# Two attention blocks: a stream's first two products interleaved, norm steps of the first attention issued later, factor operations of the projection spread over three products

## The chip, the core and the metric

The program runs on one core of a Trainium2 chip. The engines are named as the profile names them: PE (TensorE's matmuls) and PEld (its weight loads), DVE (VectorE), ACT (ScalarE), POOL (GpSimd) and SP (SyncE, which issues most of the transfers). The metric is the device time of one execution in microseconds, lower is better; a kernel's time is the median of its runs.

## The reference

The input x holds 8 images of 512 channels by 1024 positions (32 by 32), all in float32. Two layers follow each other, and each does the same five things for every image:

```
xn  = group_norm(x) * scale + bias            # 8 groups in layer 0, 32 groups in layer 1
q, k, v = qkv_w @ xn + qkv_b                  # three products of 512x512 with 512x1024
attn = softmax(q^T k / sqrt(64)) per head     # 8 heads of 64 channels
out  = attn applied to v                      # back to 512 x 1024
x    = proj_w @ out + proj_b + x              # the projection and the residual
```

## The kernel before, in words

**Units.** One layer of one image is a unit; there are 16, numbered u = 0 to 15, first the 8 images of layer 0, then those of layer 1. A unit makes v, q and k and runs its attention. The projection of a unit is done in the next unit, after that one's k; only the last is done by itself (`project_last`). Within unit u the order on PE is therefore: v, q, k of unit u, the projection o of unit u-1, the attention of unit u.

**Products in seven.** The products v, q, k and o are computed with seven block products in place of eight (2 by 2 blocks, a Strassen-like scheme), and each of these seven is again done as seven parts. `ORDER = (1, 6, 2, 7, 5, 4, 3)` is the order on both levels. The factors are sums and differences of blocks. For the weights they are stored in memory and loaded again; for the data side they are made in place by `Right.mix` (whole blocks, on DVE) and by `Right.quarter` and `Right.single` (four subtractions each, all recorded at L409: t1, t2, t4 and the in-place seventh, on POOL or DVE).

**The stream.** `Stream.product` (from L422) issues one block product. It uses two pairs of PSUM banks: a main pair (`apair[i]`, in the profile `a`), in which the four quarters q11, q12, q21 and q22 grow, and an auxiliary pair (`sbank[1-i]`, in the profile `s`), in whose bank 0 the running sum `one` grows, and in whose bank 1 lies the seventh part. i alternates from product to product. A quarter begins as a copy of `one` that ACT makes (`seed`, L444): q11 after part 1, q21 after part 6, q12 after part 5, q22 after part 4. The parts 2, 4 and 3 then add to q11, q21 and q12 (L436). ACT also copies the seventh part out of PSUM (`late`, L460); POOL adds it to results at the end (`add_late`, L480 and L489). The last two parts, 4 and 3, and the result's operations (`finish`) form a tail that is held back and issued by `close` inside the next product, after its part 1:

```
part(1, one, s, 0, True); seed(q11, 0)        # of this product
self.close()                                  # parts 4 and 3, seed q22 and finish, of the one before
part(6, ...); seed(q21, 1); part(2, ...); part(7, ...); copy late; part(5, ...); seed(q12, 0)
```

A part that adds to `one` must wait until ACT has read `one`; the parts of one product are so interleaved with the tail of the product before that another part stands between. The first product of a stream has no tail before it. There the kernel before issues the part 1 of the second product (`ahead`, only in `stream_values`) in that place, and the second product (`self.begun`) leaves its part 1 out.

**Hooks.** What DVE, POOL and SP do beside PE is placed by hand: `at(sel, k, ...)` hangs operations on the end of the result of product k of v, q, k or o. Each engine runs its instructions in the order in which they were issued. The factors of the projection are made during k: `o_part(5, ...)` are four DVE operations for the products 5 and 6 of the projection, of which `before` hangs two on k's product 7 and two on k's product 4; `o_part(4, ...)` are four POOL operations.

**Attention.** It has 64 steps (8 chunks of 8). In step s PE makes the scores (L807), ACT their exponentials (L815) into one of five tiles `p`, DVE sums those up (L852), and PE multiplies them with v (L835) one step later. Between chunks, DVE and ACT take the result out of the PSUM pair (L859, L861, L862), and DVE transposes and reduces the sums (L867, L875). `at_step` adds the group norm of the next unit: `aggregate`, `means` and `variances` (tiny matmuls, L283, into the pair that the next chunk will use, and DVE reads of them: L290 to L296, L301), the power on POOL (L303), `scales` (L308 to L318) and eight `apply` operations on ACT (L322). The steps are those of `USUAL` for u > 0 and of `LATE` for u = 0, where the input of unit 1 comes later and its statistics are taken in the attention too. `mixing` makes two of the next unit's factors on DVE (L219), `shadows` others on POOL, each tied to a summing operation of DVE. `rest_of_high` follows the attention and makes the rest of one pair's factors on POOL.

Of the kernel before, what the change touches and what calls it, by code (L numbers as in the profile page):

```python
# [11 lines left out]
F32 = mybir.dt.float32  # L12
# [6 lines left out]
P = 128  # L19
# [13 lines left out]
def fast_path(ctx, tc, x, qkv_wT, proj_wT, vecs, groups, out, flag):  # L33
# [217 lines left out]
    def halves(t):  # L251
        return [t[:, :, i : i + FD2] for i in range(0, t.shape[2], FD2)]
# [154 lines left out]
    def run(steps):  # L407
        for step in steps:
            step()  # L409

    class Stream:
# [10 lines left out]
        def product(self, a, b, keep, finish, tokens=False, ahead=None):  # L422
            i = self.n % 2
            self.n += 1
            main, aux, m, s = apair[i], sbank[1 - i], f"a{i}", f"s{1 - i}"
            one, seventh = aux[:, 0, :FD2], aux[:, 1, :FD2]
            q11, q12, q21, q22 = (main[:, r, ts(h, FD2)] for r in range(2) for h in range(2))

            def part(j, dst, tile_name, bank, start=False, a=a, b=b):
                for to, at, moving in (  # L430
                    [(dst[:, ts(i, P)], b[j][:, ts(i, P)], a[j]) for i in range(2)]
                    if tokens else [(dst, a[j], b[j])]
                ):
                    on(
                        "PE",
                        nc.tensor.matmul(  # L436
                            to, at, moving, start=start, stop=j != 1, skip_group_check=True
                        ),
                        tile_name, bank,
                    )  # L440
                    start = False

            def seed(dst, bank):
                n = nc.scalar.copy(dst, one)  # L444
                on("ACT", n, m, bank)
                on("ACT", n, s, 0)

            late = latepool.tile([P, FD2], F32, tag="late", name=f"late_{self.n}")
            if not self.begun:
                part(1, one, s, 0, True)  # L450
            self.begun = ahead is not None
            seed(q11, 0)
            if ahead is not None:
                part(1, sbank[i][:, 0, :FD2], f"s{i}", 0, True, *ahead)
            self.close()
            part(6, one, s, 0)
            seed(q21, 1)
            part(2, q11, m, 0)
            part(7, seventh, s, 1, not keep)
            on("ACT", nc.scalar.copy(late, seventh), s, 1)  # L460
            part(5, one, s, 0)
            seed(q12, 0)

            def tail():
                part(4, q21, m, 1)
                seed(q22, 1)
                part(3, q12, m, 0)
                finish(main, m, late)

            self.tail = tail  # L470
# [500 lines left out]
    def first_weights(after):  # L971
# [14 lines left out]
        "stats": (), "norm": (9, 11, 13, 16), "apply": (19, 20, 22, 23, 27, 28, 30, 31),  # L986
    }
    LATE = {
        "stats": (4, 5, 6, 7, 10, 11, 12, 13), "norm": (15, 19, 23, 26),
        "apply": (27, 28, 30, 31, 33, 35, 36, 38),  # L990
    }
    MAKING = (1, 2, 3, 4, 6)
    MAKE = {1: (1, "v"), 2: (1, "q"), 3: (1, "k"), 4: (1, "o")}
# [2 lines left out]
    for u in range(2 * B):  # L996
# [7 lines left out]
        def at(sel, k, *parts):  # L1004
            hooks.setdefault((sel, k), []).extend(parts)
# [50 lines left out]
        if u == 0:  # L1056
            def behind():
                for sel, bias, bank in (("q", QB, apair[0]), ("k", KB, sbank[1])):
                    run(block_steps(bank, lefts[sel].outer(1), right.outer[1], False, True, True))
                    t = early[sel] = ppool.tile([P, 2, FD], F32, tag="p", name=f"p1_{sel}_{u}")  # L1060

                    def copies(t=t, bank=bank, bias=bias):
                        for i in range(2):
                            nc.scalar.activation(
                                t[:, i, :], bank[:, i, :], AF.Identity, bias=vec[:, 0, bias, i : i + 1]
                            )

                    hooks[("v", 1)].insert(0, copies)

            (outer_q, inner_q), (outer_k, inner_k) = first["q"], first["k"]  # L1070
            hooks[("v", 1)].insert(1, partial(run, mixing_v[2:]))
            at("v", 6, partial(run, outer_q[:2]))
            at("v", 2, partial(run, outer_q[2:]))
            at("v", 7, partial(run, inner_q[:2]))
            at("v", 5, partial(run, inner_q[2:3]))
            at("v", 4, partial(run, inner_q[3:]), partial(store_image, 0, "q", slot_q))
            at("v", 3, partial(run, outer_k[:2]))
            at("q", 6, partial(run, outer_k[2:]))
            at("q", 2, partial(run, inner_k[:1]))
            at("q", 7, partial(run, inner_k[1:2]))  # L1080
            at("q", 4, partial(run, inner_k[2:3]))
            at("q", 3, partial(run, inner_k[3:]), partial(store_image, 0, "k", left_first_k))
            at("q", 3, partial(load_raw, 0, "o", slot_q))
            outer_o, inner_o = mix_left(slot_q)
            at("k", 7, partial(run, outer_o[:2]))
            at("k", 4, partial(run, outer_o[2:]))
            at("k", 3, partial(run, inner_o[:2]))
        else:

            (reciprocals, divide, *bias), (divide_2, *bias_2) = old.finish, old.before  # L1090
            ro = old.right_o
            o_parts = {}

            def o_rooms(ro=ro, parts=o_parts):
                tr = trpool.tile([P, 2, FD], F32, tag="tr", name=f"o_tr_{u}")
                oa, ob, oc = (ppool.tile([P, 2, FD], F32, tag="p", name=f"o{i}_{u}") for i in "abc")
                v, g = nc.vector, nc.gpsimd
                parts[1] = ro.quarter((1, 7), (*halves(tr), halves(oa)[0]), v)
                parts[5] = ro.quarter((5, 6), (halves(oa)[1], *halves(ob)), v)
                parts[2] = ro.quarter((2, 3), (*halves(oc), halves(xt[:, 1])[0]), g)  # L1100
                rooms = alone(xt[:, 1], 0, 1), alone(xt[:, 1], 1, 1), alone(xt[:, 0], 0, 0)
                parts[4] = ro.single(4, rooms, g)

            def o_part(k, lo=0, hi=4):
                return lambda: run(o_parts[k][lo:hi])

            transposed, reduced = old.sums
            at("v", 1, transposed)
            at("v", 2, reduced, divide_2)
            at("v", 4, reciprocals, bias_2[0])  # L1110
            at("v", 3, bias_2[1], o_rooms, partial(ro.mix, 0))
            at("q", 6, divide)
            at("q", 2, bias[0])
            at("q", 7, bias[1])
            at("q", 5, o_part(2, 0, 1))
            at("q", 4, partial(ro.mix, 3), o_part(2, 1, 2))
            at("q", 3, partial(ro.mix, 1))
            at("k", 1, partial(ro.mix, 2))
            at("k", 6, o_part(1, 0, 2), o_part(2, 2, 3))
            at("k", 2, o_part(1, 2), o_part(2, 3))  # L1120
            at("k", 7, o_part(5, 0, 2), o_part(4, 0, 2))
            at("k", 4, o_part(5, 2), o_part(4, 2))

        stream = Stream((u + 1) % 2)
        if u == 0:
# [48 lines left out]
        if not last:  # L1174
# [3 lines left out]
            )  # L1178
            shadows = {}
            if u == 0:  # L1180
                mixing[35], mixing[43] = partial(right.mix, 0), partial(right.mix, 1)
                parts = zip((40, 40, 42, 48, 48, 50, 56, 56), first_1 + first_6)
                parts = [*parts, *zip((58,), right.quarter((2, 3), (*halves(spare), halves(spare)[0]), nc.gpsimd))]
                for step, part in parts:
                    shadows.setdefault(step, []).append(part)
                shadows.update((at, [part]) for at, part in zip((8, 16, 24, 32), mix_left(slot_v, nc.gpsimd)[1]))
            else:
                mixing[27], mixing[35] = partial(right.mix, 0), partial(right.mix, 1)
                parts = zip((32, 32, 34, 40, 40, 42, 48, 48), first_1 + first_6)
                parts = [*parts, *zip((50, 56), right.quarter((2, 3), (*halves(spare), halves(spare)[0]), nc.gpsimd))]  # L1190
                for step, part in parts:
                    shadows.setdefault(step, []).append(part)
                if make is not None:
                    shadows.update((at, [part]) for at, part in zip((8, 16, 24), mix_left(left_slots[0], nc.gpsimd)[1][1:]))

            def rest_of_high(right=right):
                xb = ppool.tile([P, 2, FD], F32, tag="p", name=f"xb_{u + 1}")
                room, kept = halves(xb)
                run(right.quarter((2, 3), (*halves(spare), room), nc.gpsimd, kept)[1 if u == 0 else 2 :])

        making = [] if last else [None] * 8
        if make is not None:
# [332 lines left out]
```

## Time and profile before

| what | value |
|---|---|
| median of 3 runs | 3197.32 us (3197.13 to 3197.61) |
| the profiled execution, its own time | 3197.46 us |
| span of the profiled execution, first to last instruction | 3195.5 us |
| PE busy | 3170.3 us (99% of the span) |
| DVE, ACT, POOL busy | 2707.5, 2041.8 and 1257.3 us |
| mean granted TensorE clock | 0.999 |

A line of the timeline gives the start in us from the beginning of the span, the time until the last of its instructions ended, the engine, the line of the kernel, the operation, what is written and read, the shape, the number of instructions, and in brackets the idle time of the engine before it with what ended that. Matmuls are pipelined and their ends are modelled, so that the distance between two starts tells more of PE than the end of the first. A view of stretches gives the busy time of each engine with the number of its instructions, then the granted clock, the share of the DMA engines and GB/s.

### The profile page before, as it was taken

Reading aid. Unit: us, or ns where it says so; the run is one execution under the profiler, and the core shown is the slowest. Engines: PE = TensorE matmul, PEld = TensorE weight load, DVE = VectorE, ACT = ScalarE, POOL = GpSimd, SP = SyncE. Lnnn points to the kernel's source line nnn. Section 1 sums busy time; section 2 is a strip of 40 time slices with the busy share of each in tenths; the row PEclk is TensorE's granted clock in tenths of the full one; section 3 lists DMA queues with packets and bytes.
Section 4 is the critical chain, followed back from the end, with each engine's and each line's share of the span. In section 5 each row is a group of like instructions: output and inputs, shape, how many; then the busy total and the mean of one; then the engine's idle time right before and its main releaser. Section 6 shows DMA issues by size and latency. Waiting matters only on the chain.

```text
span 3195.5 us, 63766 instructions
## 1 busy us (share of the span) xinstructions
PE 3170.3 (99%) x24272; PEld 2016.2 (63%) x24272; DVE 2707.5 (85%) x3152; ACT 2041.8 (64%) x3572; POOL 1257.3 (39%) x965
## 2 busy tenths in 40 slices
PE   9999999999999999999999999999999999999999
PEld 7466484765847658476584755748567485674843
DVE  7988989889798897888979888798897988879877
ACT  3665767666676666766667666676666766667664
POOL 5145162452714427054361533615336162351620
PEclk9999999999999999999999999999999999999999
DMA  4334343443434324233142331423314233243311
GB/s 175 103 117 147 115 149 94 162 129 115 161 105 147 120 63 162 79 119 127 56 167 79 121 119 56 167 79 132 108 56 168 89 127 101 67 167 91 131 59 49
DMA packets 155270, 365.81 MB, mean 114 GB/s; under 512 B 30160, under 2 KB 45776, under 8 KB 154960
## 3 DMA queue, kind: packets, MB, share of 16 engines
q1 hardware_dynamic: 154672, 361.53, 33.9%
q8 instruction: 197, 3.23, 0.4%
q14 instruction: 113, 0.93, 0.1%
q10 hardware_dynamic: 288, 0.13, 0.0%
HBM read 299.72 MB, written 59.77 MB: 112 GB/s over the span
## 4 chain that ended last, share of the span: by engine, by line
PE 93%; DVE 4%; ACT 1%; issue 1%; DMA 0%; POOL 0%; SPq 0%; ACTq 0%; DVEq 0%; POOLq 0%
PE a L835 27%; PE s L807 25%; PE s L436 22%; PE a L436 16%; PE a L807 1%; DVE acc L852 1%; DVE ob L409 1%; ACT a L444 1%; DVE u_k L523 1%; PE s L753 0%; PE a L753 0%; PE a L409 0%; DVE oa L409 0%; DVE k L562 0%; DVE u_k L533 0%
## 5 line engine op out<-in xcount | busy, mean ns | idle before, releaser
L815 ACT ACTIVATE p<-s 128x1024 f32<-128x1024 f32 x976 | 997.0, 1023 | 524.4 <-PE s L807 499.8
L835 PE MATMUL a<-p,v 64*64 64x512 f32 x8192 | 1098.2, 590 | 4.2 <-DVE var L301 2.1
L807 PE MATMUL s<-q,k 64*64 64x512 f32 x7808 | 1056.3, 591 | 0.0
L852 DVE TENSOR_TENSOR acc<-acc,p 128x1024 f32<-128x1024 f32 x768 | 953.6, 1242 | 76.4 <-ACT p L815 35.1
L444 ACT COPY a<-s 128x256 f32<-128x256 f32 x1728 | 614.3, 358 | 326.6 <-PE s L436 220.5
L835 PEld LDWEIGHTS a<-p,v 64*64 64x64 f32 x8192 | 379.9, 131 | 505.0 <-ACT p L815 353.4
L807 PEld LDWEIGHTS s<-q,k 64*64 64x64 f32 x7808 | 377.9, 133 | 438.0 <-issue 438.0
L460 ACT COPY late<-s 128x256 f32<-128x256 f32 x432 | 160.8, 372 | 227.5 <-PE s L436 219.0
L436 PE MATMUL s<-k,w 128*128 128x256 f32 x672 | 195.2, 379 | 0.5 <-ACT a L444 0.5
L852 DVE TENSOR_TENSOR acc<-p,p 128x1024 f32<-128x1024 f32 x128 | 156.0, 1219 | 9.4 <-ACT p L815 9.4
L1249 POOL TENSOR_TENSOR k<-xn 128x256 f32<-128x256 f32 x15 | 11.0, 731 | 375.5 <-PE s L807 246.8
L867 DVE STREAM_TRANSPOSE tr<-acc 128x1024 f32<-128x1024 f32 x128 | 157.9, 1234 | 0.0
L875 DVE TENSOR_REDUCE red<-tr 128x32 f32<-128x1024 f32 x128 | 154.0, 1203 | 0.0
L436 PE MATMUL a<-xn,w 128*128 128x256 f32 x492 | 146.3, 379 | 0.0
L436 PE MATMUL a<-xt,w 128*128 128x256 f32 x462 | 137.5, 379 | 0.0
L436 PEld LDWEIGHTS s<-k,w 128*128 128x128 f32 x672 | 125.0, 190 | 19.2 <-ACT a L444 1.3
L303 POOL TENSOR_TENSOR y<-var,half 128x4 f32<-128x4 f32 (+1 forms) x17 | 17.6, 1035 | 287.4 <-DVE var L301 287.4
L862 DVE TENSOR_TENSOR ao<-a,tmp 128x512 f32<-128x512 f32 x128 | 87.9, 687 | 48.7 <-ACT tmp L861 48.1
L480 POOL TENSOR_TENSOR q<-q,late 128x512 f32<-128x512 f32 x64 | 98.4, 1537 | 62.8 <-ACT a L444 45.4
L489 POOL TENSOR_TENSOR v<-v,late 128x512 f32<-128x512 f32 x60 | 89.7, 1495 | 59.9 <-DVE v L590 35.8
L436 PE MATMUL s<-xn,w 128*128 128x256 f32 x372 | 110.7, 379 | 0.0
L436 PE MATMUL s<-xt,w 128*128 128x256 f32 x372 | 110.6, 379 | 0.0
(259 smaller groups left out, 5140.7 us busy)
## 6 DMA issues: line engine op xcount, KB each, us to landing
w<-iq SPq DMA_DIRECT2D x105, 448.0 KB, 3.4
w<-ik SPq DMA_DIRECT2D x105, 448.0 KB, 7.1
w<-io SPq DMA_DIRECT2D x105, 448.0 KB, 6.8
w<-iv SPq DMA_DIRECT2D x98, 448.0 KB, 3.9
rb<-drec SPq DMA_DIRECT2D x128, 256.0 KB, 3.9
xn<-mid SPq DMA_DIRECT2D x36, 512.0 KB, 3.6
xn<-x_dram SPq DMA_DIRECT2D x32, 512.0 KB, 3.8
res<-x_dram SPq DMA_DIRECT2D x32, 512.0 KB, 6.1
```

What stands on the lines that cost most here:

```text
L436: nc.tensor.matmul(to, at, moving, start=start, stop=j != 1, skip_group_check=True),
L444: n = nc.scalar.copy(dst, one)
L460: on("ACT", nc.scalar.copy(late, seventh), s, 1)
L480: return nc.gpsimd.tensor_add(cols, cols, twice(late))
L489: return nc.gpsimd.tensor_add(cols, cols, parts)
L807: nc.tensor.matmul(bank[e * H : (e + 1) * H, j, :], w.k[pr][j * H : (j + 1) * H, t * P + e * H : t * P + (e + 1) * H], w.q[pr][j * H : (j ...
L815: exp = nc.scalar.activation(p, bank, AF.Exp, scale=SCALE)
L835: nc.tensor.matmul(banks[r][j * H : (j + 1) * H, :], w.v[rows, t, lo : lo + D], p[rows, j, :], start=(t == 0), stop=(t == NT - 1),)
L852: state["sums"].append(nc.vector.tensor_add(acc, state["first"] if t == 1 else acc, p))
L862: i1 = nc.vector.tensor_add(ao[:, pr, ts(qh, FD)], banks[1], tmp)
L867: nc.vector.transpose(tr, state["acc"].pop(c))
L875: nc.vector.tensor_reduce(red[:, :, qh, :], state["tr"].rearrange("p j (f i) -> p j f i", i=BL), AX.X, ALU.add)
```

## The change

Three things are changed, and no instruction of the program is added or removed by them.

First, `Stream.product` has three orders in place of one. In the first product of `stream_values` (it gets `ahead`) the order is: part 1, part 7, part 1 of the second product, seed q11, copy late, part 6, seed q21, part 2, part 7 of the second product, seed q11 of the second product, part 5, seed q12. In the second product (`begun`) it is: part 6, seed q21, then the tail of the first (`close`), part 2, copy late, part 5, seed q12. All other products keep their order.

Second, for u = 0 the norm steps `means`, `variances` and `scales` come at steps 20, 27 and 30 instead of 19, 23 and 26, and the eight `apply` at 32 to 44 instead of 27 to 38. The two `mixing` operations go from 35 and 43 to 43 and 51, the eight POOL operations that follow from them from 40 to 56 to 48 to 58, and a ninth POOL operation that was tied to step 58 goes into `rest_of_high`.

Third, of the four DVE operations `o_part(5, ...)` the first stays at k's product 7, the second goes to product 4 (which keeps the third), and the fourth goes to product 3.

```diff
+            late = latepool.tile([P, FD2], F32, tag="late", name=f"late_{self.n}")
...
-            def seed(dst, bank):
+            def seed(dst, bank, one=one, m=m, s=s):
                 n = nc.scalar.copy(dst, one)
                 on("ACT", n, m, bank)
                 on("ACT", n, s, 0)
 
-            late = latepool.tile([P, FD2], F32, tag="late", name=f"late_{self.n}")
-            if not self.begun:
+            def keep_late():
+                on("ACT", nc.scalar.copy(late, seventh), s, 1)
+
+            if ahead is not None:
+
+                other, its_one, its_seventh = f"s{i}", sbank[i][:, 0, :FD2], sbank[i][:, 1, :FD2]
                 part(1, one, s, 0, True)
-            self.begun = ahead is not None
-            seed(q11, 0)
-            if ahead is not None:
-                part(1, sbank[i][:, 0, :FD2], f"s{i}", 0, True, *ahead)
-            self.close()
-            part(6, one, s, 0)
-            seed(q21, 1)
-            part(2, q11, m, 0)
-            part(7, seventh, s, 1, not keep)
-            on("ACT", nc.scalar.copy(late, seventh), s, 1)
-            part(5, one, s, 0)
+                part(7, seventh, s, 1, not keep)
+                part(1, its_one, other, 0, True, *ahead)
+                seed(q11, 0)
+                keep_late()
+                part(6, one, s, 0)
+                seed(q21, 1)
+                part(2, q11, m, 0)
+                part(7, its_seventh, other, 1, True, *ahead)
+                seed(apair[1 - i][:, 0, :FD2], 0, its_one, f"a{1 - i}", other)
+                part(5, one, s, 0)
+                self.begun = True
+            elif self.begun:
+                self.begun = False
+                part(6, one, s, 0)
+                seed(q21, 1)
+                self.close()
+                part(2, q11, m, 0)
+                keep_late()
+                part(5, one, s, 0)
+            else:
...
             seed(q12, 0)
...
     LATE = {
-        "stats": (4, 5, 6, 7, 10, 11, 12, 13), "norm": (15, 19, 23, 26),
-        "apply": (27, 28, 30, 31, 33, 35, 36, 38),
+        "stats": (4, 5, 6, 7, 10, 11, 12, 13), "norm": (15, 20, 27, 30),
+        "apply": (32, 33, 36, 38, 39, 41, 43, 44),
     }
...
-            at("k", 7, o_part(5, 0, 2), o_part(4, 0, 2))
-            at("k", 4, o_part(5, 2), o_part(4, 2))
+            at("k", 7, o_part(5, 0, 1), o_part(4, 0, 2))
+            at("k", 4, o_part(5, 1, 3), o_part(4, 2))
+            at("k", 3, o_part(5, 3))
...
             if u == 0:
-                mixing[35], mixing[43] = partial(right.mix, 0), partial(right.mix, 1)
-                parts = zip((40, 40, 42, 48, 48, 50, 56, 56), first_1 + first_6)
-                parts = [*parts, *zip((58,), right.quarter((2, 3), (*halves(spare), halves(spare)[0]), nc.gpsimd))]
+                mixing[43], mixing[51] = partial(right.mix, 0), partial(right.mix, 1)
+                parts = zip((48, 48, 50, 56, 56, 56, 58, 58), first_1 + first_6)
...
-                run(right.quarter((2, 3), (*halves(spare), room), nc.gpsimd, kept)[1 if u == 0 else 2 :])
+                run(right.quarter((2, 3), (*halves(spare), room), nc.gpsimd, kept)[0 if u == 0 else 2 :])
```

The `else` branch holds the order of before, word for word but for `keep_late()`.

More of the change, by code (lines that the diff above doesn't have):

```diff
@@ L446, in seed @@
                 on("ACT", n, s, 0)
-            late = latepool.tile([P, FD2], F32, tag="late", name=f"late_{self.n}")
-            if not self.begun:
+            def keep_late():
+                on("ACT", nc.scalar.copy(late, seventh), s, 1)
+            if ahead is not None:
+                other, its_one, its_seventh = f"s{i}", sbank[i][:, 0, :FD2], sbank[i][:, 1, :FD2]
                 part(1, one, s, 0, True)
-            self.begun = ahead is not None
-            seed(q11, 0)
-            if ahead is not None:
-                part(1, sbank[i][:, 0, :FD2], f"s{i}", 0, True, *ahead)
-            self.close()
-            part(6, one, s, 0)
-            seed(q21, 1)
-            part(2, q11, m, 0)
-            part(7, seventh, s, 1, not keep)
-            on("ACT", nc.scalar.copy(late, seventh), s, 1)
-            part(5, one, s, 0)
+                part(7, seventh, s, 1, not keep)
[18 more added lines that the diff above has]
+            else:
+                part(1, one, s, 0, True)
+                seed(q11, 0)
+                self.close()
+                part(6, one, s, 0)
+                seed(q21, 1)
+                part(2, q11, m, 0)
+                part(7, seventh, s, 1, not keep)
+                keep_late()
+                part(5, one, s, 0)
             seed(q12, 0)
```

## The prediction

> **What bounds the kernel now.** I read the page's busy times first, then the list of waits for PE, then the timelines of three places that PE's starts point to.
>
> ```profile
> PE 3170.3 (99%) x24272; PEld 2016.2 (63%) x24272; DVE 2707.5 (85%) x3152; ACT 2041.8 (64%) x3572; POOL 1257.3 (39%) x965
> ```
>
> PE sets the time: whatever closes a hole between its matmuls is won whole, and nothing else is. The waits of PE say where holes are:
>
> ```profile
> PE s L436 <- ACT a L444: 4.2, 17, 0.5
> PE a L835 <- DVE var L301: 2.1, 1, 2.1
> PE a L835 <- ACT p L815: 2.0, 1, 2.0
> ```
>
> These are too small, as ends of matmuls are modelled; I go by starts. First place, the start of a stream (unit 3; PE, then the ACT copy that it waits for):
>
> ```profile
> 595.20 0.71 PE L436 MATMUL s<-w,xn 128*128 128x128 f32 x4
> 595.75 0.61 PE L436 MATMUL s<-w,xt 128*128 128x128 f32 x4
> 596.50 0.68 PE L436 MATMUL s<-w,k 128*128 128x128 f32 x4
> 597.02 0.61 PE L436 MATMUL a<-w,xn 128*128 128x128 f32 x4
> ...
> 598.36 0.61 PE L436 MATMUL a<-w,k 128*128 128x128 f32 x4
> 599.03 0.71 PE L436 MATMUL a<-w,xn 128*128 128x128 f32 x4
> ...
> 601.36 0.61 PE L436 MATMUL s<-w,xn 128*128 128x128 f32 x4
> ...
> 596.00 0.36 ACT L444 COPY a<-s 128x256 f32<-128x256 f32 x1 [2.10 <-PE s L436]
> ```
>
> A part (a line here) takes 0.447 us when nothing waits (597.02 to 598.36 are three of them). The twelve parts from 595.20 to 601.36 should take 5.36, plus 0.10 for the slow first one, and take 6.16: 0.70 is lost. Of it 0.38 lie at 596.50 (part 6 waits until ACT has read `one`, then restarts slowly) and 0.32 at 599.03 (part 3 waits for seed q12). All 15 streams of u > 0 show it: 0.70 in thirteen, 0.98 in units 11 and 12.
>
> Second place, the end of k (unit 3; DVE, ACT, PE):
>
> ```profile
> 653.91 0.67 DVE L409 TENSOR_TENSOR oa<-ot 128x512 f32<-128x512 f32 x1
> 654.62 1.64 DVE L409 TENSOR_TENSOR ob<-ot,oa 128x512 f32<-128x512 f32 x1
> 656.18 0.68 DVE L533 TENSOR_TENSOR u_k<-a,u_k 128x512 f32<-128x512 f32 x1
> 656.78 0.67 DVE L562 TENSOR_TENSOR k<-a,u_k 128x512 f32<-128x512 f32 x1
> ...
> 657.55 0.63 ACT L444 COPY a<-s 128x256 f32<-128x256 f32 x2 [0.68 <-DVE k L562]
> ...
> 657.17 0.59 PE L436 MATMUL a<-xt,w 128*128 128x256 f32 x2
> 657.96 0.70 PE L436 MATMUL s<-spare,w 128*128 128x256 f32 x2 [0.19 <-ACT a L444]
> ```
>
> PE needs 0.43 per part here; 657.17 to 657.96 is 0.79, and the next part starts 0.10 late: 0.46 lost. Backwards: seed q11 of product 3 waits for DVE to read product 5's bank 0 (L562), which queues behind the second factor operation, 1.64 us long. This too stands in each of the 15 units.
>
> Third place, the attention of u = 0 (PE, ACT, then a view of stretches):
>
> ```profile
> 125.84 1.13 PE L807 MATMUL s<-q,k 64*64 64x512 f32 x8
> 129.11 1.09 PE L835 MATMUL a<-p,v 64*64 64x512 f32 x8 [2.14 <-DVE var L301]
> ...
> 135.14 1.07 PE L807 MATMUL s<-q,k 64*64 64x512 f32 x8
> 138.24 1.47 PE L835 MATMUL a<-p,v 64*64 64x512 f32 x8 [2.03 <-ACT p L815]
> ...
> 136.37 0.81 ACT L322 ACTIVATE xn<-xn,shift,scale 128x512 f32<-128x512 f32 x1 [2.51 <-DVE shift L318]
> ...
> 138.00:143.00 5.00, 4.76 (x30) 1.93 (x34) 3.94 (x5) 3.19 (x5) 0.00 (x0) 0.66 0.01 3
> ```
>
> From its first scores to the next stream this attention takes 116.87 us, the others 110.26 to 110.35: 6.5 lost. 2.4 are the products of step 24, whose bank DVE has not yet read for the variances; 2.2 the exponential behind an `apply` that waits for `shift`; 1.7 a stretch of half clock right after (granted 0.66 over 138 to 143); 0.2 later.
>
> **The parts and their costs.**
>
> *Stream start.* No instruction is added. Copy to refill: part 1 starts at 595.20, ACT copies at 596.00 for 0.36, PE resumes at 596.50, so 1.30 after part 1's start (1.20 for later parts). Now two parts stand between (7 and the other 1): part 6's turn comes at 0.10 + 3 x 0.447 = 1.44. Part 5's copy feeds part 3 two parts later in the same way, margin 0.14. The new seed q11 of the second product stands in ACT's queue behind seed q21: part 6 starts at 1.44, seed q21 runs 2.14 to 2.50, the new one to 2.86, PE may go on at 3.00, its turn is at 3.23. That copy writes the pair that DVE empties last (L859, L862); they end 1.55 after the stream's start in every unit, 0.95 before it is due. Behind it in ACT's queue are q12, q21, q22 and the copy of v's first result; all keep at least 0.1. So 0.70 x 15 = 10.5 gained; the extra 0.28 of units 11 and 12 I leave as noise (11.1 with it). Unhidden at worst: one of the hops again, about 0.3 per start, 4.5.
>
> *Factor operations.* The 1.64 us operation moves from before product 5's result to after product 4's. L533 then starts when product 5's tail is done, near 654.8, not 656.18. L562 also needs POOL's add to u_k (done 655.71 by its row, 654.07 for 1.64), so bank 0 is read by 656.5, and the ACT copy is due at 656.9, after part 1 of product 3. The hole of 0.46 closes: 15 units sum to 7.0. What is later: L409 twice after product 4's result (ends 658.9), then product 3's result, then the fourth operation. They take 0.67 alone and up to 1.75 beside POOL (its adds are 1.27 each). Two such give 662.4 at worst, against 662.25, where product 3's result stands now, and the copy of the projection's product 6 that needs this result comes near 664.2. The fourth operation ends by 665.5 at worst; its reader, part 7 of that product 6, comes near 661.1 - 0.46 + 3.02 + 5 x 0.43 = 665.8. All is covered, by 0.3 at worst, 1.9 if no POOL operation is in the way. Cost 0, bounds -0.46 (the gain eaten) and 0 per unit.
> The Trainium skill, page "SBUF — State Buffer", section "Who interferes with whom", says a DVE instruction with two SBUF inputs and a GpSimd one that reads SBUF block each other for a whole instruction; 0.67 against 1.64 to 1.75 in this trace agrees. By that rule all three moved operations could draw the long time, the worst case just given.
>
> *First attention.* Matmul of the means one step later: DVE reads them before the products of step 25, since its pair is free until then. Variances at step 27, in chunk 3, use the pair of chunk 4, whose products start at step 33: the 2.4 goes. DVE, however, is behind by 3 us and stays the clock of `scales`. From its rows: sums 1.33 apart, 1.14 before another operation, reciprocals 1.56, transposition 1.16, reduction 1.13, divide 1.14, means 0.54. From step 20's sum (121.93): means at 123.07, step 24's evacuation at 128.9, sum of step 27 at 134.4, variances 135.5 (step 33's products come after 140: free), step 30's sum 139.2, `shift` done 141.35. Step 32's scores come at 124.08 + 8 x 1.718 = 137.82, its exponential ends at 140.0, the evacuation copy at 140.54, so `apply` waits 0.8 for `shift`, ends 142.2, the next exponential 143.1, and products that were due at 142.1 start at 143.3: 1.15 lost, with two more `apply` in a row 0.15. So 6.5 - 1.3 = 5.2 gained; bounds 6.5 (DVE catches up, ACT alone costs little) and 2.5 (DVE 1 us later and half clock again).
> The Trainium skill, page "TensorE: Matmul & The Clock Gate", section "What's actually happening", has the clock halved after an idle window of about 3.4 us; here two idles of about 2.2, neither of that length, came before the 0.66, so the trace is stricter. By the page one hole of 1.15 leaves the clock whole, as I took it.
> `mixing` and POOL's work come later in u = 0. The last eight small operations (0.74 each) end near step 60, before unit 1 reads them. The ninth starts without its tie: DVE sums beside POOL rows take 2.11 in place of 1.23 (192 to 199), one or two more of them use up DVE's idle 1.06 before L859 of unit 1. I take 0.3, bounds 0 and 1.0.
>
> *Sum.* Against the profiled execution's own 3197.46 (span 3195.5 and 1.96 around it, 0.14 above the median): -10.5 - 7.0 - 5.2 + 0.3 = -22.4, 3175.1. Against the median it is 3174.9; I say 3175.0.
>
> **Rivals.**
> 1. *The first attention still jams.* For: DVE's backlog, and step 32 puts evacuation copy and `apply` on ACT together. Against: the variance read is off the path. Gain 2.5 or less, worst none: 3177.7 to 3180.5.
> 2. *DVE and POOL block each other, and product 3's result or the fourth factor comes late:* the 0.46 moves into the projection. For: the 0.3 margin at worst. Against: POOL must draw first three times. 3182.
> 3. *The streams keep one hop,* as margins of 0.14 are thin. Against: the ordinary products run on the same margin without holes. 10.5 - 4.5 gained: 3179.5.
> 4. *Slower than before:* the new seed q11 is issued before q12 and the rest on ACT; if it waits for more of DVE than the emptying, all behind it waits. It decides when DVE's release comes later than 2.6 after the start (then part 6 of the second product is late), and turns the sum when it costs 22.4/15 = 1.5 per start, so at 4.1. If it waited for the first factor of the next mix (L219, ends 5.15), 2.5 x 15 = 38: 3213. Against: L862 ends at 1.55 fifteen times.
> 5. *Nothing changes,* as PE waits elsewhere for the same engines: 3197.
>
> **Chances.** Forecast 0.62 (3173 to 3177.5), rival 1 0.15, rival 2 0.09, rival 3 0.08, rival 4 0.04, rival 5 0.02. The low end takes all bounds: 11.1 + 7.1 + 6.5 = 24.7, 3172.5. The high end includes rivals 1 to 3: 3182.5. Within 0.2% (6.4 us, about what a measurement here can tell from no change) is rival 5 and the edge of 4: 0.03; slower 0.04; faster 0.93.
>
> **What would show it.** After: PE's streams start their second `s<-w,xn` after 5.46, with no idle before parts 6 and 3; at the end of k no ACT wait for L562, `ob` after L551; the first attention near 111.6 with one wait for ACT around step 33, none for var, and no stretch under full clock. Wrong if the streams still take 6.16, if a hole of 0.4 opens in the projection, or if unit 0 keeps more than 114.

## The result, and the profile after

The changed kernel takes 3176.12 us (median of 4 runs, 3175.14 to 3177.38) against 3197.23 (3196.84 to 3197.61) for the kernel before: a ratio of 0.9934, 95% interval 0.9917 to 0.9951. The forecast was 3175.0, with a range from 3172.5 to 3182.5. The profiled execution has a span of 3175.5 us, 20.0 less than that of before. A second series (e10_after below) gave 3174.88, ratio 0.9932 (0.9918 to 0.9946).

The page's first part, of the changed kernel:

```profile
PE 3159.3 (99%) x24272; PEld 2027.4 (64%) x24272; DVE 2686.2 (85%) x3152; ACT 2043.6 (64%) x3572; POOL 1261.4 (40%) x965
```

The same instructions on every engine, as the diff says. The waits of PE, those that answer to the three of before:

```profile
PE a L858 <- ACT p L838: 2.3, 1, 2.3
PE s L437 <- ACT a L445: 1.9, 3, 0.9
```

The wait for `var` is gone. Of 17 waits of `s` for ACT's copies three are left (L437 is the old L436, L445 the old L444, L858 the old L835, L838 the old L815, L830 the old L807, L875 the old L852, L882 and L885 the old L859 and L862, L574 and L585 the old L551 and L562).

The start of a stream, unit 3, PE in order of time (start, time until the last ended, what, how many):

```profile
591.61 1.16 PE L437 MATMUL s<-w,xn 128*128 128x128 f32 x8
592.61 0.61 PE L437 MATMUL s<-w,xt 128*128 128x128 f32 x4
593.05 0.61 PE L437 MATMUL s<-w,k 128*128 128x128 f32 x4
593.50 0.61 PE L437 MATMUL a<-w,xn 128*128 128x128 f32 x4
593.95 1.50 PE L437 MATMUL s<-w,k 128*128 128x128 f32 x12
595.29 0.61 PE L437 MATMUL a<-w,k 128*128 128x128 f32 x4
595.73 0.61 PE L437 MATMUL a<-w,xn 128*128 128x128 f32 x4
...
597.07 0.61 PE L437 MATMUL s<-w,xn 128*128 128x128 f32 x4
```

The first line is parts 1 and 7 together, the fifth parts 7 (of the second product), 5 and 6 (of the second). From 591.61 to the third product's first part at 597.07 it takes 5.46 us, where it took 6.16: not one start is late. The end of k, unit 3, DVE and PE:

```profile
649.63 0.68 DVE L409 TENSOR_TENSOR oa<-ot 128x512 f32<-128x512 f32 x1
650.49 0.69 DVE L556 TENSOR_TENSOR u_k<-a,u_k 128x512 f32<-128x512 f32 x1 [0.19 <-PE a L437]
651.10 0.68 DVE L585 TENSOR_TENSOR k<-a,u_k 128x512 f32<-128x512 f32 x1
...
653.63 1.23 DVE L574 TENSOR_TENSOR k<-a,u_k 128x1024 f32<-128x1024 f32 x1 [0.65 <-PE a L437]
654.77 0.68 DVE L409 TENSOR_TENSOR ob<-ot,oa 128x512 f32<-128x512 f32 x1
655.49 1.64 DVE L409 TENSOR_TENSOR ob<-ot,ob 128x512 f32<-128x512 f32 x1
657.05 1.21 DVE L574 TENSOR_TENSOR k<-a,u_k 128x1024 f32<-128x1024 f32 x1
658.18 0.77 DVE L409 TENSOR_TENSOR ot<-ot 128x512 f32<-128x512 f32 x1
...
652.88 0.64 PE L437 MATMUL a<-xt,w 128*128 128x256 f32 x2
653.36 0.59 PE L437 MATMUL s<-spare,w 128*128 128x256 f32 x2
```

Product 5's result (L556, the old L533) now waits for PE and no longer behind the factor operation; L585 reads bank 0 by 651.78. On PE 652.88 to 653.36 is 0.48 where it was 0.79. Of the three operations that now stand at the products 4 and 3, all of which run beside rows of POOL, one took 1.64 (the others 0.68 and 0.77), here and in the 14 other units.

The first attention: PE, then ACT and one line of DVE, then three stretches (length, busy time and instructions of PE, PEld, DVE, ACT and POOL, granted clock, DMA share, GB/s):

```profile
142.13 1.13 PE L830 MATMUL s<-q,k 64*64 64x512 f32 x8
145.57 1.09 PE L858 MATMUL a<-p,v 64*64 64x512 f32 x8 [2.31 <-ACT p L838]
...
140.78 0.58 ACT L884 COPY tmp<-a 128x512 f32<-128x512 f32 x1
143.70 0.81 ACT L322 ACTIVATE xn<-xn,shift,scale 128x512 f32<-128x512 f32 x1 [2.34 <-DVE shift L318]
144.42 1.00 ACT L838 ACTIVATE p<-s 128x1024 f32<-128x1024 f32 x1
...
125.53 0.59 DVE L914 TENSOR_REDUCE tot<-lt 32x64 f32<-32x256 f32 x1 [0.98 <-DMA lt<-red]
```

```profile
138.00:143.00 5.00, 5.00 (x51) 2.36 (x42) 4.86 (x8) 2.52 (x3) 2.00 (x1) 1.00 0.02 3
143.00:148.00 5.00, 2.69 (x28) 1.12 (x28) 4.90 (x9) 4.30 (x6) 2.10 (x1) 1.00 0.00 0
148.00:153.00 5.00, 5.00 (x52) 2.10 (x48) 4.79 (x5) 4.22 (x6) 0.00 (x0) 1.00 0.06 12
```

One hole is left, at step 33 and for the reason given: `apply` on ACT waits for `shift`. The clock stays whole. This execution lost 2.5 us there; 1.0 of it is DVE's wait for a landing (`lt<-red`), which is absent in the other profiles of this order. From its scores to the next stream this attention took 112.84 us here and 111.78 in e10_after, against 116.87 before.

What the forecast had too small stands at the start of unit 1, DVE, POOL, ACT and PE:

```profile
191.50 8.25 DVE L875 TENSOR_TENSOR acc<-acc,p 128x1024 f32<-128x1024 f32 x4
199.67 0.68 DVE L882 COPY tmp<-a 128x512 f32<-128x512 f32 x1
200.38 0.69 DVE L885 TENSOR_TENSOR ao<-a,tmp 128x512 f32<-128x512 f32 x1
...
191.99 2.26 POOL L409 TENSOR_TENSOR spare<-xn 128x512 f32<-128x512 f32 x1
194.32 2.14 POOL L409 TENSOR_TENSOR spare<-xn,spare 128x512 f32<-128x512 f32 x1
196.54 2.13 POOL L409 TENSOR_TENSOR xb<-xn,spare 128x512 f32<-128x512 f32 x1
198.63 2.25 POOL L409 TENSOR_TENSOR xb<-xn 128x512 f32<-128x512 f32 x1
...
201.11 0.63 ACT L445 COPY a<-s 128x256 f32<-128x256 f32 x2 [1.38 <-DVE ao L885]
...
201.52 0.71 PE L437 MATMUL s<-w,k 128*128 128x128 f32 x4 [0.90 <-ACT a L445]
```

DVE's last four sums take 8.25 us beside four operations of POOL. So DVE empties the pair 3.85 us after the stream began (200.38 + 0.69 - 197.23), the copy q11 of the second product waits for that, and PE loses 1.16 there and 1.0 more in v. Unit 1 takes 198.30, the usual unit 196.08.

One hole stands in every unit of the kernel before and of the changed one alike. PE at the end of unit 3's projection:

```profile
675.81 0.59 PE L437 MATMUL s<-oc,w 128*128 128x256 f32 x2
676.24 0.59 PE L437 MATMUL a<-xt,w 128*128 128x256 f32 x2
676.85 0.70 PE L437 MATMUL a<-ao,w 128*128 128x256 f32 x2
```

From 676.24 to 676.85 it takes 0.61 in place of 0.43, and the last part restarts 0.10 late: 0.28 lost. The order is part 5, copy q12, part 4, part 3, with one part between the copy and the part that adds to it, as in the second hole of the old stream start. In the 15 units with a projection it adds up to 4.2 us, and no run here changes it.

### The profile page after: what moved, and what is told of

The parts are those of the page before. It is cut to its first block, busy times and chain, and to the rows that moved or that the text cites. A ratio compares the mean times of both kernels' runs of the same rounds, so it can differ in the third digit from the quotient of the medians.

```text
span 3175.5 us, 63781 instructions
## 1 busy us (share of the span) xinstructions
PE 3159.3 (99%) x24272; PEld 2027.4 (64%) x24272; DVE 2686.2 (85%) x3152; ACT 2043.6 (64%) x3572; POOL 1261.4 (40%) x965
## 4 chain that ended last, share of the span: by engine, by line
PE 97%; DVE 1%; DMA 0%; issue 0%; ACT 0%; SPq 0%; DVEq 0%; ACTq 0%
PE a L858 27%; PE s L830 26%; PE s L437 23%; PE a L437 18%; PE a L830 1%; DVE acc L875 1%; PE s L776 0%; PE a L776 0%; PE a L409 0%; PE s L345 0%; PE s L409 0%; DVE w L409 0%; DMA xn<-x_dram 0%; DMA rb<-drec 0%; DMA drec<-rec 0%
## 5 line engine op out<-in xcount | busy, mean ns | idle before, releaser
L838 ACT ACTIVATE p<-s 128x1024 f32<-128x1024 f32 x976 | 997.2, 1023 | 520.7 <-PE s L830 497.7
L858 PE MATMUL a<-p,v 64*64 64x512 f32 x8192 | 1100.4, 589 | 2.3 <-ACT p L838 2.3
L830 PE MATMUL s<-q,k 64*64 64x512 f32 x7808 | 1058.6, 590 | 0.0
L875 DVE TENSOR_TENSOR acc<-acc,p 128x1024 f32<-128x1024 f32 x768 | 955.7, 1244 | 75.8 <-ACT p L838 32.9
L445 ACT COPY a<-s 128x256 f32<-128x256 f32 x1728 | 616.1, 358 | 324.1 <-PE s L437 225.2
L858 PEld LDWEIGHTS a<-p,v 64*64 64x64 f32 x8192 | 382.6, 131 | 499.1 <-ACT p L838 353.4
L830 PEld LDWEIGHTS s<-q,k 64*64 64x64 f32 x7808 | 383.5, 133 | 431.5 <-issue 431.5
L437 PE MATMUL s<-k,w 128*128 128x256 f32 x672 | 195.3, 380 | 0.5 <-ACT a L445 0.5
L875 DVE TENSOR_TENSOR acc<-p,p 128x1024 f32<-128x1024 f32 x128 | 156.1, 1220 | 9.0 <-ACT p L838 9.0
L437 PE MATMUL a<-xn,w 128*128 128x256 f32 x492 | 146.5, 379 | 0.0
L437 PE MATMUL a<-xt,w 128*128 128x256 f32 x462 | 137.5, 379 | 0.0
L437 PEld LDWEIGHTS s<-k,w 128*128 128x128 f32 x672 | 125.1, 190 | 19.1 <-ACT a L445 1.3
L885 DVE TENSOR_TENSOR ao<-a,tmp 128x512 f32<-128x512 f32 x128 | 88.1, 688 | 48.7 <-ACT tmp L884 48.2
L437 PE MATMUL s<-xn,w 128*128 128x256 f32 x372 | 110.7, 379 | 0.0
L437 PE MATMUL s<-xt,w 128*128 128x256 f32 x372 | 110.7, 379 | 0.0
L322 ACT ACTIVATE xn<-xn,shift,scale 128x512 f32<-128x512 f32 x124 | 99.5, 804 | 14.2 <-DVE shift L318 14.2
```

The lines of the kernel that those rows point to most:

```text
L322: nc.scalar.activation(cols, cols, AF.Identity, bias=st["shift"][:, c - lo : c - lo + 1], scale=st["scale"][:, c - lo : c - lo + 1],)
L437: nc.tensor.matmul(to, at, moving, start=start, stop=j != 1, skip_group_check=True),
L830: nc.tensor.matmul(bank[e * H : (e + 1) * H, j, :], w.k[pr][j * H : (j + 1) * H, t * P + e * H : t * P + (e + 1) * H], w.q[pr][j * H : (j ...
L838: exp = nc.scalar.activation(p, bank, AF.Exp, scale=SCALE)
L858: nc.tensor.matmul(banks[r][j * H : (j + 1) * H, :], w.v[rows, t, lo : lo + D], p[rows, j, :], start=(t == 0), stop=(t == NT - 1),)
L875: state["sums"].append(nc.vector.tensor_add(acc, state["first"] if t == 1 else acc, p))
```

## The experiments

**The three parts by themselves.** Each is the kernel before with one part of the diff: the new `product` and no more, the three lines of `o_part(5, ...)` and no more, the `LATE`, `mixing`, `parts` and `rest_of_high` lines and no more.

> The kernel before with the new stream order alone. My theory: the two holes of each stream (0.38 and 0.32) close in all 15 units, unit 1 too, because without the later POOL work of unit 0 DVE empties the pair in time: 10.5 to 11.1 us less than before, 3186.2 to 3186.7 against a before of 3197.2. The rival (the copy q11 of the second product waits for DVE, which empties that pair last): a hole like the 1.06 us one of unit 1 would stand in more units, 3188 or more. Streams should take 5.46 us from the first part to the third product's first part.

> The kernel before with the projection's factor operations over three products alone. My theory: the hole of 0.46 at the end of k closes in all 15 units and nothing opens in the projection: 7.0 us less, 3190.2. The rival (DVE and POOL block each other, and the hole moves on): 3197 or up to 3194, with holes of some tenths in the projection.

> The kernel before with the later norm steps of the first attention alone (with their later mixing and POOL operations). From the changed kernel's trace: the attention of unit 0 loses 2.5 in place of 6.5, 4.0 won; unit 1 starts with DVE 2.3 us late, which in the old stream order costs nothing at the copy q11 of the second product (it is due later there) but about 0.9 in v: 3.1 less, 3194.1. If instead the 2.1 us that unit 1 lost belong to the norm steps whatever the stream order, 1.9 less, 3195.3. If half clock returns, 1.7 more.

| kernel | median (runs) | before, same chips | ratio (95%) | what its profile shows |
|---|---|---|---|---|
| e1_stream | 3186.10 (6) | 3197.5 (27) | 0.9965 (0.9952 to 0.9977) | a usual unit 196.55 (197.25 before); no hole at any of the 15 starts |
| e2_factors | 3189.41 (10) | 3197.5 (27) | 0.9976 (0.9966 to 0.9985) | a usual unit 196.78; no hole at the end of k, and in the projection only the 0.28 at its end that before has too |
| e3_norm | 3193.76 (10) | 3197.5 (27) | 0.9989 (0.9980 to 0.9999) | attention of unit 0 111.81, with one hole of 1.5; unit 1 198.35, 1.0 more than before |

The three gains are 11.4, 8.1 and 3.7 us by the medians, 23.2 together, where the whole change gave 21.1 and 22.7 in its two series. By the profiles the 15 starts take 11.3 less (93.2 to 81.9), the factor operations gain 7.1, the norm steps 4.1. For e1_stream that agrees with the theory, unit 1 included: without the later norm steps the pair is emptied in time there. For e3_norm, too, the first of the two accounts holds: the norm steps cost unit 1 1.0 us in the old order of the stream, and 1.4 to 2.2 together with the new one.

**Half of the interleave.** In the kernel before, only the first product's part 7 is moved:

```diff
             seed(q11, 0)
             if ahead is not None:
+                part(7, seventh, s, 1, not keep)
                 part(1, sbank[i][:, 0, :FD2], f"s{i}", 0, True, *ahead)
...
             part(2, q11, m, 0)
-            part(7, seventh, s, 1, not keep)
+            if ahead is None:
+                part(7, seventh, s, 1, not keep)
```

> The kernel before, but the first product of a stream issues its part 7 second; the second product keeps its old order. My theory of two separate holes: the one ahead of part 6 closes (0.38), the one ahead of part 3 stays (0.32): 15 x 0.38 = 5.7 less, 3191.5, and 5.78 from a stream's first part to the third product. The rival, that the first hole is only passed on to the second: same as before.

3195.38 us (10 runs), ratio 0.9993 (0.9983 to 1.0003): the expected 5.7 did not come. PE at the start of unit 5 of this kernel:

```profile
990.15 1.16 PE L436 MATMUL s<-w,xn 128*128 128x128 f32 x8
991.14 0.61 PE L436 MATMUL s<-w,xt 128*128 128x128 f32 x4
991.59 0.61 PE L436 MATMUL s<-w,k 128*128 128x128 f32 x4
992.04 0.61 PE L436 MATMUL a<-w,xn 128*128 128x128 f32 x4
992.70 0.71 PE L436 MATMUL s<-w,k 128*128 128x128 f32 x4
993.25 0.61 PE L436 MATMUL a<-w,k 128*128 128x128 f32 x4
993.92 0.71 PE L436 MATMUL a<-w,xn 128*128 128x128 f32 x4
...
996.25 0.50 PE L436 MATMUL s<-w,xn 128*128 128x128 f32 x3
```

The hole ahead of part 6 is closed (991.14 to 991.59), but a new one has opened ahead of part 5 (992.04 to 992.70, 0.32 with its slow restart), and the one ahead of part 3 stays (993.25 to 993.92). Part 7 had been the second of the two parts that cover the copy q21; taken away, it was missed there. The start takes 6.10 instead of 6.16. So the rival came close to the truth, by another way than it said: the copies q11, q21 and q12 each need two parts of 0.447 between. The change gives q21 its second only because the second product's part 7 takes the place that the first one's left, and q12 its second by the second product's part 6.

**Is the third product needed?** The changed kernel with the fourth factor operation on product 4 again:

```diff
-            at("k", 4, o_part(5, 1, 3), o_part(4, 2))
-            at("k", 3, o_part(5, 3))
+            at("k", 4, o_part(5, 1), o_part(4, 2))
```

> The changed kernel, but the fourth factor operation hangs on k's product 4 with the second and third (two products instead of three, with only one on product 7). Theory: what closed the hole at the end of k is that the long operation left product 7; the fourth one at product 4 delays only product 3's result, by up to 1.75, to just when the projection needs it: same as the changed kernel within 0.5 us, at most 0.1 per unit. The rival, that the third step is needed: holes of 0.3 or more per unit in the projection, 3180 or more.

3184.49 us (5 runs), ratio to before 0.9960 (0.9947 to 0.9974), about 9 more than the changed kernel: the rival was right. DVE, ACT and PE in unit 5:

```profile
1050.88 1.21 DVE L409 TENSOR_TENSOR ot<-ot 128x512 f32<-128x512 f32 x1
1052.02 1.21 DVE L574 TENSOR_TENSOR k<-a,u_k 128x1024 f32<-128x1024 f32 x1
...
1053.32 0.63 ACT L445 COPY a<-s 128x256 f32<-128x256 f32 x2 [0.82 <-DVE k L574]
...
1052.80 0.59 PE L437 MATMUL a<-ao,w 128*128 128x256 f32 x2
1053.72 0.48 PE L437 MATMUL s<-ob,w 128*128 128x256 f32 x1 [0.33 <-ACT a L445]
```

The fourth operation stands ahead of product 3's result (L574), which comes 1.13 later than in the changed kernel, and the copy for the projection's product 6 waits 0.82 for it. PE loses 0.59 in each of the 15 units (8.9), more than the hole that the other move had closed. In the changed kernel L574 ends some 0.4 before that copy is due (1050.73 against 1051.14 in unit 5).

**The loss in unit 1.** The changed kernel with the mixing operations earlier and the POOL operations at their old steps, the ninth tied to step 58 again; run twice, the second time beside the changed kernel.

```diff
-                mixing[43], mixing[51] = partial(right.mix, 0), partial(right.mix, 1)
-                parts = zip((48, 48, 50, 56, 56, 56, 58, 58), first_1 + first_6)
+                mixing[39], mixing[46] = partial(right.mix, 0), partial(right.mix, 1)
+                parts = zip((40, 40, 42, 48, 48, 50, 56, 56), first_1 + first_6)
+                parts = [*parts, *zip((58,), right.quarter((2, 3), (*halves(spare), halves(spare)[0]), nc.gpsimd))]
...
-                run(right.quarter((2, 3), (*halves(spare), room), nc.gpsimd, kept)[0 if u == 0 else 2 :])
+                run(right.quarter((2, 3), (*halves(spare), room), nc.gpsimd, kept)[1 if u == 0 else 2 :])
```

> The changed kernel, but the mixing operations of unit 0 at steps 39 and 46, and the POOL operations at their old steps (40 to 56, and the ninth tied to step 58 again). Theory: the 2.1 us that unit 1 loses come from POOL's big operations running beside DVE's last sums, so that DVE empties the pair 2.3 us late; with the old places the hole of 1.06 and that of 0.7 go, unit 1 takes 196.1 to 196.3 instead of 198.3: 3174.1 against 3176.1. The rival (the backlog comes from the later norm steps themselves): unit 1 stays near 198.

> The changed kernel once more, as the measure for the other runs of this chip: 3176.1 as before; the attention of unit 0 with one hole of 1.5 us in place of the 2.5 of its first profile, where a landing was late; unit 1 near 198.3.

> The kernel with the mixing operations at 39 and 46 and POOL at its old steps once more, beside the changed kernel: 1.8 us less than the changed kernel, all of it in unit 1 (196.5 against 198.3). If the gain of its first run was the scatter between chips, no difference.

e4_tied: 3173.55 us (5 runs), ratio 0.9928 (0.9915 to 0.9942). On another chip e10_after 3174.88 (5 runs) and e11_tied 3174.68 (5 runs, ratio 0.9929, 0.9915 to 0.9943). By the time the two cannot be told apart; by the profile they can: unit 1 takes 198.30 and 197.44 in the two profiles of the changed kernel, 196.52 and 196.17 in the two of the tied one (whose second loses 0.75 in unit 2 instead). So the loss is about 1, not 2, and lies within the runs' scatter. The edit moves two DVE operations along with POOL's, so the times alone would not say which of them mattered; the rows of the last four sums do, e11_tied first, then e10_after:

```profile
188.84 7.16 DVE L875 TENSOR_TENSOR acc<-acc,p 128x1024 f32<-128x1024 f32 x4
188.64 8.27 DVE L875 TENSOR_TENSOR acc<-acc,p 128x1024 f32<-128x1024 f32 x4
```

In e11_tied they take 1.11 less, about the 7.14 of the kernel before: POOL is at work beside all four in e10_after (189.13 to 198.03), and pauses for 1.25 in e11_tied. So the cause is the one that the theory names, POOL's operations beside DVE's last sums, at about half the price it gave.

**Where a hole goes.** Three kernels on top of the tied order. e5_both:

```diff
-        "apply": (32, 33, 36, 38, 39, 41, 43, 44),
+        "apply": (36, 38, 39, 41, 42, 44, 45, 46),
...
-                mixing[39], mixing[46] = partial(right.mix, 0), partial(right.mix, 1)
+                mixing[43], mixing[47] = partial(right.mix, 0), partial(right.mix, 1)
```

e9_less is e5_both without unit 0's division in chunk 5 (`asum`, into whose columns the divisions sum, is set to 1 by a memset at the start); that part of its result stays undivided:

```diff
-            if c % NH == 1 and t == 5 and c > 1 and (c < n_chunks - 1 or final):
+            if c % NH == 1 and t == 5 and c > 1 and (c < n_chunks - 1 or final) and (u or c != 5):
```

e8_best is the tied order with `scales` one step earlier and unit 0's last evacuation copy on ACT:

```diff
-        "stats": (4, 5, 6, 7, 10, 11, 12, 13), "norm": (15, 20, 27, 30),
+        "stats": (4, 5, 6, 7, 10, 11, 12, 13), "norm": (15, 20, 27, 29),
...
-            if c == n_chunks - 1 and not final:
+            if c == n_chunks - 1 and not final and u:
```

> As the run before it, and also the eight apply at steps 36 to 46, with the mixing operations at 43 and 47. Theory: the hole of 2.5 us in the first attention is ACT waiting at step 32 for the shift that DVE delivers late; four steps later nothing waits: the attention of unit 0 falls from 112.8 to 110.4, and the whole to about 3171.7. The rival (ACT alone is too full for eight more operations): holes of some tenths remain at each pair of apply, 3173.

> The kernel with apply at 36 to 46, and one DVE operation of unit 0 left out: the division by the softmax sums in chunk 5 (1.14 us; that part of unit 0's result is not divided). Theory: the holes at unit 1's start (1.55) and in its v (0.7) are nothing but DVE's backlog at the end of unit 0, so the first falls by 1.1 to about 0.45, the second to a half or less, and unit 1 from 198.8 to 197.2 or less, with the attention still without a hole. The rival (POOL's operations beside the last sums set it alone): no change.

> As the run before it, with the scales at step 29 instead of 30, and for unit 0 the last evacuation copy on ACT instead of DVE. Theory (DVE's backlog is what sets unit 0): shift comes one sum (1.33 us) earlier, so the hole at step 33 falls from 1.46 to about 0.3; the 1.1 us that DVE no longer gets as a gift appear at its end, and the copy taken off it gives 0.7 back there: unit 1 at most 196.9. In all 0.5 to 1 less than the tied kernel. The rival (backlog only moves): same as the tied kernel.

e5_both: 3175.27 us (5 runs), ratio 0.9931 (0.9918 to 0.9945), not the expected 3171.7. e8_best: 3175.04 (5 runs), 0.9932 (0.9919 to 0.9946), not the expected 0.5 to 1 less than the tied order (3174.68 beside it). e9_less: one run, 3174.86. In the profiles the hole of the attention is gone in all three (110.30, 110.46 and 110.30 us), and it has come back in unit 1. "Emptied" is the end of DVE's last read of the pair (L885) after the start of unit 1's stream, the hole is that ahead of the second product's part 6, less the slow restart of 0.10:

| profile | attention of unit 0 | emptied | hole at the start | unit 1 | the two units' sum |
|---|---|---|---|---|---|
| e11_tied | 111.83 | 1.59 | 0 | 196.17 | 308.00 |
| e4_tied | 111.81 | 2.04 | 0 | 196.52 | 308.33 |
| e10_after | 111.78 | 2.98 | 0.19 | 197.44 | 309.22 |
| e8_best | 110.46 | 3.32 | 0.53 | 198.36 | 308.82 |
| e9_less | 110.30 | 3.60 | 0.82 | 198.07 | 308.37 |
| after | 112.84 | 3.85 | 1.06 | 198.30 | 311.14 |
| e5_both | 110.30 | 4.34 | 1.55 | 198.81 | 309.11 |

In every row with a hole, emptied less hole is 2.78 or 2.79: PE waits for DVE one to one from there on. And attention and unit 1 together stay within 1.2 us of each other (the first profile of the changed kernel, with its late landing, apart), while the first moves by 1.5 and the second by 2.6. In e5_both DVE is busy for 106.6 of the attention's 110.30 us, and it empties the pair at 4.34 in place of the 1.55 of before: it has more to do there than it finishes while PE does not wait. A hole that PE loses in the middle is time in which DVE catches up; closed there, it opens at the end. The division left out (1.14) brought the emptying forward by 0.74 and the whole by as much, not by the 1.6 expected: the later hole in v stays at 0.69 as long as there is a first one, since that first one brings PE back to DVE's distance. What became of the other 0.4 stays open. No version was shown to beat the changed kernel.

## Why the prediction was right, point by point

*Stream start* (10.5, or 11.1 with two units' extra): right. All 15 starts take 5.46 in the profile of e1_stream, so the two holes' 10.5 are gone, and the margin of 0.14 held everywhere. The other 0.8 are slips: the 0.28 of units 11 and 12, and 0.21 in unit 10, whose start takes 6.38 and not the 6.16 that the prediction gives to thirteen units. They are absent from the starts of e6_half too, which keep their holes, so it is not shown that the change removed them.

*Factor operations* (7.0, nothing after it): right in size, 7.1 by the profile of e2_factors. But one step of its cover was wrong: the copy that needs product 3's result was put near 664.2, 1.8 after the worst case, and the fourth operation's reader at 665.8. I had taken the projection's part 6 (`s<-o_tr`, 661.08) for its part 1, which is `s<-ao` at 659.79; all that is counted from there is 1.3 too late. The real margin was some 0.4, and e7_two, which used the supposed one, cost 8.9. That nothing was lost after it was in part luck: of the two operations ahead of product 3's result one took 1.64 and the other 0.68. Had both been long, the result would have come 0.96 later; where it came 1.13 later (e7_two) PE stood 0.49 us and restarted slowly, so an estimate of the loss is 0.3 to 0.4 per unit. By the exclusive lock between DVE and POOL that the Trainium skill's page "SBUF — State Buffer", section "Who interferes with whom", describes, all three operations could have been slow; one was (1.64).

*First attention* (5.2): right to 0.2 in five of six profiles (111.8 for 116.87). `shift` was forecast for 141.35 in the old profile's clock; where no landing was late it came at 141.69 with an almost equal start (e10_after). The extra 1.0 in the first profile is the wait for `lt<-red`, 0 in the eight other profiles with these norm steps. With the old ones DVE stands still before the same instruction for 0.95 in e2_factors and 1.47 in e6_half, and not at all in before and e1_stream.

*Unit 1* (0.3, bounds 0 and 1.0): mis-sized, 1.36 and 2.2. The step said that one or two more of DVE's sums would be slowed and use up an idle 1.06. The sums were sized rightly: the last four took 7.14 before and 8.25 to 8.27 after, 1.1 more. What failed is the idle time that was to pay for it. In before DVE has 1.06 left at the end because PE loses 6.5 us on the way; in the changed kernel PE loses 1.5 there (2.5 in the first profile), so DVE comes to the end later against it. e11_tied shows it: its last sums take 7.16, as in before, and yet DVE has no idle time after them, and the pair is emptied at 1.59, as in before (1.55). So the 1.1 of the sums came on top (2.98 in e10_after). Rival 4 named the place and the price of what then happened, a new copy q11 behind DVE's emptying, with 2.6 as the point where it begins; measured is 2.79, and in one unit of 15. The later hole in v (0.69) was in no term.

*The sum* was 1.1 us off the first series and 0.1 off the second. That it came so near is partly luck: the terms as measured, 10.5 + 7.1 + 5.1 - 1.4, give 21.3, not 22.4, and the rest of the second series' 22.7 is slips and late landings that differ between executions, in a series that runs from 3174.16 to 3176.86. One of them, 0.78 where DVE waited for a landing (`rb<-drec`), stands in unit 10 of the profile of before and in unit 15 of both profiles of the changed kernel.

## What to carry to other kernels

When PE waits for a copy that another engine makes of its result, count the parts between the writer and the next one that overwrites; moving one of them to fill a hole may take it from another. A hole on the bottleneck engine is rest for the one next to it: where that one is nearly full, closing the hole moves it, and what counts is the sum over the stretch up to the point where the second engine has caught up. And an operation that is moved "off the path" needs the due time of whatever queues behind it, counted from the right line of the trace.

## What the runs showed of the hardware

Whether the clock halves depends on how the idle time falls. The clock records in these traces change to half only at whole multiples of 3.413 us from their first record, and a slow stretch in the middle lasts one such window. Cut along these windows, PE's idle time in unit 0, by the modelled ends of its matmuls, was:

| profile | idle in us, by window | half clock in the next window |
|---|---|---|
| e6_half | 1.60 + 2.10 | yes, after the 2.10 |
| e1_stream | 1.17 + 0.95; later 2.04 | no; yes |
| before | 1.61 + 0.53; later 2.03 | no; yes |
| e2_factors | 1.97 + 1.20; later 1.94 + 0.09 | no; no |
| after | 0.50 + 1.81 | no |
| e3_norm, e4_tied | 1.29 and 1.28 | no |

An idle stretch of 3.17 us (e2_factors) left the clock at 1.00, one of 2.03 (before) halved it: what decides in these traces is whether one window holds more than about 2.0 us of idle time (1.97 did not halve it, 2.03 did). The ends of all 13 traces, where PE stops, agree: the first window there with 2.45 us or more of idle time is followed by half clock, and the one ahead of it, with 1.54 or less, is not. The two stretches of e2_factors and e6_half, in the same columns as above:

```profile
131.00:134.50 3.50, 3.50 (x37) 1.47 (x33) 3.50 (x3) 1.63 (x2) 2.12 (x2) 1.00 0.04 12
```

```profile
131.10:134.60 3.50, 3.50 (x24) 1.49 (x28) 3.50 (x3) 1.02 (x1) 2.90 (x2) 0.68 0.14 32
```

In equal time PE issued 37 matmuls in the first and 24 in the second. The prediction had read the trace as stricter than the Trainium skill's page "TensorE: Matmul & The Clock Gate", section "What's actually happening" (halved after at least one idle window of about 3.4 us); the windows of that length agree, the wholly idle window does not.
